# Softmax weights transposed unscaled; the inverse row sums multiplied in after the value product

## The chip, the core and the metric

The kernel runs on one core of a Trainium2 chip. The metric is device time in microseconds (us) of one launch, from several runs of the same program. Beside the times there is one profiled execution, from which the trace and its page come. The engines have short names: PE (matrix products; PEld is its loading of weights), DVE (VectorE), ACT (ScalarE), POOL (GpSimd), SP (the queue that issues nearly all DMAs here). The 16 DMA engines move data between SBUF and DRAM and within SBUF.

## What is computed

The reference is two blocks, both float32, on x of 4 x 1024 x 512: a graph attention over 20 key positions with a ReLU and a residual, and then a conditioned transformer block. The change touches the attention of the second:

```
def _attention(x, W_qkv, W_out, b_out):          # B=4, 16 heads of 64, here 1024 rows
    q, k, v = jnp.split(x @ W_qkv, 3, axis=-1)   # each reshaped to (B, T, 16, 64)
    attn = jnp.einsum('bqhd,bkhd->bhqk', q, k) * DH ** -0.5
    attn = jax.nn.softmax(attn, axis=-1)
    out = jnp.einsum('bhqk,bkhd->bqhd', attn, v).reshape(Bq, Tq, INNER)
    return out @ W_out + b_out
x = x + g_msa * _attention(_modulate(_layernorm(x), sh_msa, sc_msa), W_qkv, W_out, b_out)
x = x + g_mlp * _ff(_modulate(_layernorm(x), sh_mlp, sc_mlp), W1, b1, W2, b2)
```

## The kernel before

There are three stages: the graph attention (to about 408 us), the softmax attention with the projections around it (408 to about 2230 us), and the feed-forward stage. All engines' instructions are emitted by the program in a fixed order; each engine takes its own in that order, and semaphores make it wait where it needs another's result.

The softmax stage is a loop over 256 steps (`for s in range(NS + 1)`). A step is one batch, one pair of heads (`gp`, 8 of them) and one tile `t` of 128 query rows (8 of them). In a step:

- `scores` (L1156): PE writes the scores of the two heads, 128 x 1024 each, into two PSUM tiles `psc`.
- `largest` (L1167): DVE reduces each to its negated row maximum.
- `weights` (L1173): ACT takes the exponential of each into `w`, and the row sums `sm` with it.
- `scaled`: DVE takes the reciprocal of each sum (L1178), and then ACT (head 0, L1180) or POOL (head 1, L1182) multiplies the 128 x 1024 weights by it, in place.
- `turn` (L1191, L1195): DVE transposes the weights in blocks of 32 x 32 into `wd`, and after every second tile SP issues four DMAs of 256 KB for each head, which move the blocks of `wd` between partitions into `wT`. Eight DMAs belong to one block of `QB` = 256 query rows, that is two steps; there are 128 such blocks. `wd` has three slots, and a block takes two of them, one for each head; `wT` has two slots.
- `attend` (L1064, L1076): at least two steps after the second tile, PE multiplies `wT` with the values into the PSUM tile `pav`, and ACT copies `pav` into `oT`, which is the input of the output projection.

The weights of step s are transposed in step s+1: `turn` of head 0 is the first thing that DVE does in it, and `turn` of head 1 stands behind the two maxima and the first reciprocal. Before the maxima stand the evacuations that the step before put off (`later`).

The rest of the step is filled by `emit`. A planner gives every piece of other work (projections to queries, keys and values in seven products, L533; the output projection, L1139 with DVE's additions in L1148; `attend`; loads of weights and rows) a cost and a first and last step, and spreads them so that the steps are about equally long on PE. The planner and its costs are the same in both kernels. Loads (`wqk`, `wv`, `wout`, `xr`, `xl`) and stores (`x2d`) of these pieces go through SP's queue too, in the order of emission. The program waits for a DMA by semaphore on the engine that needs it; where SP needs the landing of a DMA before it issues another, SP waits and so does everything behind it.

Of the kernel before, what the change touches and what calls it, by code (L numbers as in the profile page):

```python
# [12 lines left out]
F32 = mybir.dt.float32  # L13
I32 = mybir.dt.int32
AF = mybir.ActivationFunctionType
ALU = mybir.AluOpType
# [3 lines left out]
P = 128  # L20
S = 1024
F = 512
FC = F // P
NT = S // P
# [8 lines left out]
H, D = 16, 64  # L33
# [8 lines left out]
def cond_block_kernel(  # L42
# [27 lines left out]
    nc = tc.nc  # L70
# [4 lines left out]
    def row(ap):  # L75

        return ap.unsqueeze(0)
# [46 lines left out]

    x1d = [tc.dram_tile([P, F], F32, name=f"x1d{i}") for i in range(NTA)]
    gated = tc.dram_tile([P, F], F32, name="gated")
    qrd = tc.dram_tile([B, F], F32, name="qrd")
    vrd = [tc.dram_tile([KV, F], F32, name=f"vrd{d}") for d in range(2)]
    x2d = [tc.dram_tile([P, F], F32, name=f"x2d{i}") for i in range(NTA)]
# [2 lines left out]
    with ExitStack() as gctx:  # L132
        KC0 = GH * 2 * NG // P
        HF = GH * NG
        gp = gctx.enter_context(tc.tile_pool(name="gp", bufs=1))
# [49 lines left out]
        with ExitStack() as sctx:  # L185
# [13 lines left out]
            rows = sp.tile([N_VEC, P], F32, name="rows")  # L199
# [8 lines left out]
            ws, gboB = [], sp.tile([KV, 2, F], F32, name="gboB")  # L208
# [365 lines left out]
        later = []  # L574
# [366 lines left out]
    with ExitStack() as actx:  # L941
        ap_ = actx.enter_context(tc.tile_pool(name="ap", bufs=1, reuse_waits="tile"))
        q1, q2 = (ps.tile([P, F], F32, name=n, tag=n) for n in ("q1", "q2"))
        two_banks = {"ma": q2, "mb": q1, "mc": q1, "md": q2}
        NP = 2 * NGRP
# [3 lines left out]
        QB = 256  # L949
        QT = QB // P  # L950
        NB = S // QB
        wout, gate = {}, {}
        vt, oT, xr, wn, wd, wT = {}, {}, {}, {}, {}, {}

        turns = []

# [98 lines left out]
        def attend(b, gp, k, a=0, z=KC):  # L1055

            if a == 0:
                pav[0] = ps.tile([P, F], F32, name="pav", tag="pav")[:, :QB]
            po = pav[0]
            g, p = divmod(gp, 2)  # L1060
            w = wT[b, gp, k]
            for m in range(a, z):
                for j in range(2):
                    nc.tensor.matmul(  # L1064
                        po[j * D : (j + 1) * D, :],
                        lhsT=vt[b, g][:, m, p * P + j * D : p * P + (j + 1) * D],
                        rhs=w[:, j, :, m, :],
                        start=(m == 0),
                        stop=(m == KC - 1),
                    )  # L1070
            if z < KC:
                return
            u, i = divmod(k, 2)
            if i == 0:
                oT[b, gp, u] = op_.tile([P, F], F32, name="oT", tag="oT", bufs=6)
            nc.scalar.copy(  # L1076
                oT[b, gp, u][:, i * QB : (i + 1) * QB].rearrange("p (t u q) -> p u t q", t=QT, u=4),
                po.rearrange("p (u t q) -> p u t q", t=QT, u=4),
            )

        def project(b, g, n):
# [69 lines left out]
        def scores(b, gp, t):  # L1151
            sc = [ps.tile([P, S], F32, name="psc", tag="sc", bufs=2) for _ in range(2)]
            for n in range(2):
                for j in range(2):
                    q = slice(j * D, (j + 1) * D)
                    nc.tensor.matmul(  # L1156
                        sc[j][:, n * F : (n + 1) * F],
                        lhsT=qT[b, gp][q, t * P : (t + 1) * P],
                        rhs=kT[b, gp][q, n * F : (n + 1) * F],
                        start=True,  # L1160
                        stop=True,
                    )
            return sc

        def largest(sc):
            mx = ap_.tile([P, 1], F32, name="mx", tag="mx", bufs=4)
            nc.vector.tensor_reduce(mx, sc, axis=AX.X, op=ALU.max, negate=True)  # L1167
            return mx

        def weights(sc, mx):  # L1170
            w = ap_.tile([P, S], F32, name="w", tag="w", bufs=4)
            sm = ap_.tile([P, 1], F32, name="sm", tag="sm", bufs=4)
            nc.scalar.activation(w, sc, AF.Exp, bias=mx, accum_out=sm)  # L1173
            return w, sm

        def scaled(j, w, sm):

            nc.vector.reciprocal(sm, sm)  # L1178
            if j == 0:
                nc.scalar.mul(w, w, sm)  # L1180
            else:
                nc.gpsimd.tensor_scalar(w, w, sm, None, ALU.mult)  # L1182

        def turn(b, gp, t, j):

            k, at = divmod(t, QT)
            if at == 0:
                wd[j] = ap_.tile([P, 4 * KC, QT, U], F32, name="wd", tag="wd", bufs=3)
                if j == 0:
                    wT[b, gp, k] = ap_.tile([P, 2, 4, KC, QT * U], F32, name="wT", tag="wT", bufs=2)  # L1190
            nc.vector.transpose(wd[j][:, :, at, :], wn.pop((b, gp, t, j)).rearrange("p (m k) -> p m k", k=U))  # L1191
            if at == QT - 1:
                flat = wd[j].rearrange("p m t q -> p (m t q)")
                for u in range(4):
                    nc.sync.dma_start(  # L1195
                        wT[b, gp, k][:, j, u].rearrange("p m q -> p (m q)"), flat[U * u : U * (u + 1), :]
                    )
# [11 lines left out]
        def halves():  # L1209

            two = [ps.tile([P, S], F32, name="up", tag="sc", bufs=2) for _ in range(2)]
            return {n: two[k // 2][:, k % 2 * F : (k % 2 + 1) * F] for k, n in enumerate(("ma", "mb", "mc", "md"))}
# [5 lines left out]
        NS = B * NP * NT  # L1218
# [21 lines left out]
        for b in range(B):  # L1240
# [22 lines left out]
            for gp in range(NP):  # L1263
                g, p = divmod(gp, 2)
                at = s0 + gp * NT
# [12 lines left out]
                for k in range(NB):  # L1278
                    lo = at + QT * k + LAG
                    if gp == NP - 2:  # L1280

                        for h in range(2):
                            add(lo + h, lo + h, 1, 1, attend, b, gp, k, h * KC // 2, (h + 1) * KC // 2)
                        continue
                    add(lo, lo + (lo < NS - 8), 2, 1, attend, b, gp, k)
# [60 lines left out]
        for i in range(4):  # L1346
            at = NS - (10, 9, 6, 3)[i]
# [109 lines left out]
        def fill_of(s):  # L1457
            return [k for k in range(len(fill)) if where[k] == s]

        def emit(a, b):  # L1460


            for s in range(a, b):
                steps = {where[k] for k in chain}
                second = [k for k in outs if where[k] == s][1:]

                def place(k):
                    if k in inside:
                        at = 2.5 if s - 1 in steps else 0.5
                        if k in chain:  # L1470
                            return at
                        if k in second:
                            return 3.5
                        return min(at, 2) + 0.1 if s in steps else 2
                    return fill[k][3]

                for k in sorted(fill_of(s), key=lambda k: (place(k), k)):
                    if k not in done_early:
                        fill[k][4]()
                if s in steps and s - 1 not in steps and sum(fill[k][2] for k in fill_of(s)) >= 3:  # L1480
                    while later:
                        later.pop(0)()
# [3 lines left out]
        def early(s):  # L1486

            two = [k for k in outs if where[k] == s]
            sums = [k for k in fill_of(s) if fill[k][3] == -1]
            for k in two[: len(two) - 1] + sums:  # L1490
                fill[k][4]()
                done_early.add(k)

        row_sum(0, 2)
        emit(-3, 0)
        before = None
        for s in range(NS + 1):
            if before is not None:
                turn(*before[0], 0)
            while later:  # L1500
                later.pop(0)()
            if s < NS:
                b, r = divmod(s, NP * NT)
                gp, t = divmod(r, NT)
                sc = scores(b, gp, t)
                mx = [largest(sc[j]) for j in range(2)]
                early(s)
                ws = [weights(sc[j], mx[j]) for j in range(2)]
                now = ((b, gp, t), ws)
                scaled(0, *ws[0])  # L1510
            if before is not None:
                turn(*before[0], 1)
            before = None
            if s < NS:
                scaled(1, *ws[1])
                for j in range(2):
                    wn[(*now[0], j)] = ws[j][0]
                before = now
            if s < NS:
                emit(s, s + 1)  # L1520
        sc_banks = halves()
        late = []
        second = with_four(
# [25 lines left out]
    with ExitStack() as mctx:  # L1549
# [53 lines left out]
        for k in range(NB2):  # L1603
            b = k * VB // NT
# [3 lines left out]
            for p in range(2 if k == 0 else 0, 4):  # L1608
# [12 lines left out]
                elif p == 3:  # L1621
                    sums = []
                    for j in range(2):
                        o = [w2x[j][:, n] for n in range(3)]
                        q, r = w2s[j], w2s[2 + j]
# [97 lines left out]
```

## Time and profile before

| | us |
|---|---|
| runs | 3037.86, 3039.97, 3045.48 |
| median | 3039.97 |
| span of the profiled execution | 3034.2 |
| first softmax step to last exponential | about 408 to 2230 |
| L1182, POOL's scaling pass, 256 of them | 728.6 busy |
| L1180, ACT's scaling pass, 256 of them | 291.0 busy |
| L1178, DVE's reciprocals, 512 of them | 72.5 busy |
| L1076, ACT's copies of `pav`, 128 of them | 0.352 / 0.359 / 0.373 each (least, median, most) |

A group of the page reads: line, engine, operation, what it writes and reads, how many, then busy time and mean ns of one, then the idle time of the engine just before these instructions, and what ended most of it. In a view of waits the first name is the engine and line that waited (SPq is SP's queue), then whom it waited for, then the sum, the count and the longest. The slices of the page for PE's granted clock and for the DMA engines over the whole span, and SP's part of the DMA queues:

```profile
PEclk9999999999999999999999999999999999999999
DMA  6433357777868777768777868766871010101110
...
q1 hardware_dynamic: 282256, 415.03, 53.8%
...
wT<-wd SPq DMA_DIRECT2D x1024, 256.0 KB
```

A digit is a slice of a fortieth of the span. The clock is at full speed throughout, and the DMA engines are busiest in the softmax stage, where the 1024 transfers of `wT` lie.

### The profile page before, as it was taken

How to read it: one execution, taken by the hardware profiler on the slowest of the kernel's cores; microseconds unless marked ns; L12 is line 12 of the kernel's file. 1: busy time of each engine (PE TensorE's matmuls, PEld its weight loads, DVE VectorE, ACT ScalarE, POOL GpSimd, SP SyncE). 2: the span in 40 equal slices, each digit the busy share in tenths (PEclk: the TensorE clock that was granted, in tenths of full speed). 3: DMA queues.
4: the chain of work that ended last, by engine and by line, in shares of the span. 5: the costliest groups of instructions: out<-in, count | busy, mean ns of one | idle time of the engine just before them, and what ended most of it. 6: DMA issues, size and time to landing. Idle time of an engine off the chain costs nothing.

```text
span 3034.2 us, 41780 instructions
## 1 busy us (share of the span) xinstructions
PE 2999.3 (99%) x15317; PEld 1980.2 (65%) x15317; DVE 1999.6 (66%) x2836; ACT 1432.0 (47%) x2368; POOL 1339.4 (44%) x922
## 2 busy tenths in 40 slices
PE   9999999999999999999999999999999999999999
PEld 6666655555555555555555555555568888888888
DVE  3888867777878877878787878877863222222322
ACT  3344456555755565755555755556641221112211
POOL 1444456555656655656655656655721110111010
PEclk9999999999999999999999999999999999999999
DMA  6433357777868777768777868766871010101110
GB/s 201 140 118 121 117 129 180 162 171 179 192 157 210 181 168 179 192 155 211 187 159 180 191 159 205 189 162 164 203 196 63 14 49 28 49 21 35 35 42 15
DMA packets 282695, 417.90 MB, mean 138 GB/s; under 512 B 28968, under 2 KB 101092, under 8 KB 282492
## 3 DMA queue, kind: packets, MB, share of 16 engines
q1 hardware_dynamic: 282256, 415.03, 53.8%
q8 instruction: 123, 2.02, 0.3%
q14 instruction: 80, 0.66, 0.1%
q10 hardware_dynamic: 236, 0.20, 0.0%
HBM read 120.93 MB, written 25.76 MB: 48 GB/s over the span
## 4 chain that ended last, share of the span: by engine, by line
PE 83%; DVE 7%; ACT 3%; POOL 3%; issue 2%; DMA 2%; SPq 1%; POOLq 0%; DVEq 0%; ACTq 0%
PE q L533 19%; PE psc L1156 15%; PE pav L1064 13%; PE pu L1139 6%; PE mbd L533 5%; PE mbu L533 5%; PE mad L533 4%; PE mau L533 3%; PE mcd L533 2%; PE mdd L533 2%; PE mdu L533 2%; PE mcu L533 2%; DVE mx L1167 1%; ACT w L1173 1%; POOL t L742 1%
## 5 line engine op out<-in xcount | busy, mean ns | idle before, releaser
L1182 POOL TENSOR_SCALAR w<-w,sm 128x1024 f32<-128x1024 f32 x256 | 728.6, 2846 | 701.5 <-DVE sm L1178 686.4
L1173 ACT ACTIVATE w<-psc,mx 128x1024 f32<-128x1024 f32 x512 | 570.7, 1115 | 642.6 <-DVE mx L1167 641.6
L1191 DVE STREAM_TRANSPOSE wd<-w 128x1024 f32<-128x1024 f32 x512 | 632.2, 1235 | 109.3 <-ACT w L1180 96.0
L1167 DVE TENSOR_REDUCE mx<-psc 128x1 f32<-128x1024 f32 x512 | 599.2, 1211 | 80.2 <-PE psc L1156 77.0
L1156 PE MATMUL psc<-kT,qT 64*128 64x512 f32 x2048 | 526.9, 615 | 3.1 <-ACT kT L1024 1.4
L1064 PE MATMUL pav<-wT,v 128*64 128x256 f32 x4096 | 482.1, 383 | 1.2 <-DMA wT<-wd 0.6
L1064 PEld LDWEIGHTS pav<-wT,v 128*64 128x64 f32 x4096 | 296.1, 137 | 224.0 <-issue 86.0
L1156 PEld LDWEIGHTS psc<-kT,qT 64*128 64x128 f32 x2048 | 201.6, 186 | 220.5 <-issue 151.2
L1180 ACT ACTIVATE w<-w,sm 128x1024 f32<-128x1024 f32 x256 | 291.0, 1137 | 0.0
L512 POOL TENSOR_TENSOR tx<-hT 128x512 f32<-128x512 f32 x8 | 10.3, 1288 | 596.5 <-ACT hT L448 596.5
L1148 DVE TENSOR_TENSOR xr<-pu,xr 128x512 f32<-128x512 f32 x210 | 143.5, 683 | 78.9 <-PE pu L1139 78.7
L533 PE MATMUL q<-hT,wqk 128*128 128x512 f32 (+1 forms) x396 | 181.2, 581 | 1.0 <-DVE q L547 1.0
L555 ACT COPY mbu<-mau 128x512 f32<-128x512 f32 x30 | 17.1, 570 | 276.5 <-PE mau L533 276.5
L719 PE MATMUL pa<-kp,sfT 128*128 128x320 f32 x512 | 143.5, 433 | 1.4 <-ACT sfT L694 1.4
L533 PEld LDWEIGHTS q<-hT,wqk 128*128 128x128 f32 x396 | 74.7, 190 | 80.9 <-issue 78.2
L533 PE MATMUL q<-tx,ex 128*128 128x512 f32 (+1 forms) x264 | 123.5, 591 | 1.8 <-POOL tx L618 1.3
L719 PEld LDWEIGHTS pa<-kp,sfT 128*128 128x128 f32 x512 | 94.8, 190 | 38.2 <-ACT sfT L694 1.9
L679 PE MATMUL pf<-wx,xT 128*128 128x512 f32 x256 | 116.0, 596 | 0.0
L533 PE MATMUL mad<-w,hs 128*128 128x256 f32 x512 | 113.1, 379 | 0.0
L533 PEld LDWEIGHTS mad<-w,hs 128*128 128x128 f32 x512 | 97.3, 190 | 13.2
L1139 PE MATMUL pu<-wout,oT 128*128 128x256 f32 x360 | 98.4, 396 | 4.2 <-DVE xr L1148 3.7
L1139 PEld LDWEIGHTS pu<-wout,oT 128*128 128x128 f32 x360 | 62.6, 189 | 59.3 <-issue 31.6
(309 smaller groups left out, 4590.7 us busy)
## 6 DMA issues: line engine op xcount, KB each, us to landing
wT<-wd SPq DMA_DIRECT2D x1024, 256.0 KB
wqk<-in_w_qkv SPq DMA_DIRECT2D x64, 256.0 KB
xT<-in_xt SPq DMA_DIRECT2D x32, 256.0 KB
xs<-in_x SPq DMA_DIRECT2D x32, 256.0 KB
x1d<-xs SPq DMA_DIRECT2D x32, 256.0 KB
xl<-x1d SPq DMA_DIRECT2D x32, 256.0 KB
wv<-in_w_qkv SPq DMA_DIRECT2D x32, 256.0 KB
xr<-x1d SPq DMA_DIRECT2D x32, 256.0 KB
```

The source lines that it names most:

```text
L533: nc.tensor.matmul(t[:, q * width : (q + 1) * width], lhsT=lhs(which, q, k), rhs=rhs(which, q, k), start=(fresh and q == 0 and k == 0), st ...
L679: nc.tensor.matmul(pfs[i], lhsT=xT[i][:, c, :], rhs=wx[:, c, :], start=False, stop=(c == FC - 1), skip_group_check=True,)
L719: nc.tensor.matmul(pas[i][:, n, :HF], lhsT=sfT2[i][:, c, :], rhs=kp[:, b, c, n * HF : (n + 1) * HF], start=False, stop=(c == FC - 1), skip ...
L1064: nc.tensor.matmul(po[j * D : (j + 1) * D, :], lhsT=vt[b, g][:, m, p * P + j * D : p * P + (j + 1) * D], rhs=w[:, j, :, m, :], start=(m == 0),
L1139: nc.tensor.matmul(pu[0][:, q * HB : (q + 1) * HB], lhsT=a[:, q * P : (q + 1) * P], rhs=r, start=(bool(fresh) and q == 0), stop=True, skip ...
L1148: nc.vector.tensor_tensor(o, pu[0].rearrange("p (r f) -> p r f", r=2), o, ALU.add)
L1156: nc.tensor.matmul(sc[j][:, n * F : (n + 1) * F], lhsT=qT[b, gp][q, t * P : (t + 1) * P], rhs=kT[b, gp][q, n * F : (n + 1) * F], start=Tru ...
L1167: nc.vector.tensor_reduce(mx, sc, axis=AX.X, op=ALU.max, negate=True)
L1173: nc.scalar.activation(w, sc, AF.Exp, bias=mx, accum_out=sm)
L1180: nc.scalar.mul(w, w, sm)
L1182: nc.gpsimd.tensor_scalar(w, w, sm, None, ALU.mult)
L1191: nc.vector.transpose(wd[j][:, :, at, :], wn.pop((b, gp, t, j)).rearrange("p (m k) -> p m k", k=U))
```

## The change

The weights keep their raw exponentials. The scaling passes are gone. The row sums of the two tiles and two heads of a block gather in one tile of 128 x 4; after the second tile DVE inverts them in one instruction (`scales_out`) and SP stores them to DRAM, turned, as four rows of 128. In the next step SP reads them back (`scales_in`), once for each head, as a row of 256 spread over that head's 64 partitions, into `rB`. `attend` then leaves PSUM by a DVE multiplication with `rB` instead of an ACT copy. The transposes move too: `turn` of both heads now stands in the same step, behind the exponentials, and `w` has two slots instead of four.

```diff
+    scd = [tc.dram_tile([4, P], F32, name=f"scd{i}") for i in range(4)]
...
-            nc.scalar.copy(
+            nc.vector.tensor_tensor(
                 oT[b, gp, u][:, i * QB : (i + 1) * QB].rearrange("p (t u q) -> p u t q", t=QT, u=4),
                 po.rearrange("p (u t q) -> p u t q", t=QT, u=4),
+                rB.pop((b, gp, k)).rearrange("p (t u q) -> p u t q", t=QT, u=4),
+                ALU.mult,
             )
...
-        def weights(sc, mx):
-            w = ap_.tile([P, S], F32, name="w", tag="w", bufs=4)
-            sm = ap_.tile([P, 1], F32, name="sm", tag="sm", bufs=4)
-            nc.scalar.activation(w, sc, AF.Exp, bias=mx, accum_out=sm)
-            return w, sm
-        def scaled(j, w, sm):
+        def weights(b, gp, t, j, sc, mx):
+            k, at = divmod(t, QT)
+            w = ap_.tile([P, S], F32, name="w", tag="w", bufs=2)
+            if (b, gp, k) not in esum:
+                esum[b, gp, k] = ap_.tile([P, 2 * QT], F32, name="sm", tag="sm", bufs=2)
+            c = j * QT + at
+            nc.scalar.activation(w, sc, AF.Exp, bias=mx, accum_out=esum[b, gp, k][:, c : c + 1])
+            wn[b, gp, t, j] = w
+        def scales_out(b, gp, k):
+            sm = esum.pop((b, gp, k))
             nc.vector.reciprocal(sm, sm)
-            if j == 0:
-                nc.scalar.mul(w, w, sm)
-            else:
-                nc.gpsimd.tensor_scalar(w, w, sm, None, ALU.mult)
+            spot[0] += 1
+            scales[b, gp, k] = scd[spot[0] % len(scd)]
+            nc.sync.dma_start(scales[b, gp, k].rearrange("c p -> p c"), sm)
+        def scales_in(b, gp, k):
+            rows = scales.pop((b, gp, k))
+            rB[b, gp, k] = ap_.tile([P, QB], F32, name="rB", tag="rB", bufs=2)
+            for j in range(2):
+                nc.sync.dma_start(
+                    rB[b, gp, k][j * D : (j + 1) * D, :],
+                    row(rows[j * QT : (j + 1) * QT, :].rearrange("t q -> (t q)")).broadcast_to([D, QB]),
+                )
...
-        for s in range(NS + 1):
-            if before is not None:
-                turn(*before[0], 0)
+        for s in range(NS):
             while later:
                 later.pop(0)()
...
+            for j in range(2):
+                weights(b, gp, t, j, sc[j], mx[j])
+            for j in range(2):
+                turn(b, gp, t, j)
+            while coming:
+                scales_in(*coming.pop())
+            if t % QT == QT - 1:
+                scales_out(b, gp, t // QT)
+                coming.append((b, gp, t // QT))
+            emit(s, s + 1)
```

More of the change, by code (lines that the diff above doesn't have):

```diff
@@ L953, in cond_block_kernel @@
         vt, oT, xr, wn, wd, wT = {}, {}, {}, {}, {}, {}
+        esum, scales, rB, spot = {}, {}, {}, [0]
         turns = []
@@ L1495, in cond_block_kernel @@
         emit(-3, 0)
-        before = None
-        for s in range(NS + 1):
-            if before is not None:
-                turn(*before[0], 0)
+        coming = []
+        for s in range(NS):
             while later:
                 later.pop(0)()
[L1502 to L1520, printed above, removed]
+            b, r = divmod(s, NP * NT)
+            gp, t = divmod(r, NT)
+            sc = scores(b, gp, t)
+            mx = [largest(sc[j]) for j in range(2)]
+            early(s)
+            for j in range(2):
[8 more added lines that the diff above has]
+            emit(s, s + 1)
+        while later:
+            later.pop(0)()
+        scales_in(*coming.pop())
         sc_banks = halves()
```

## The prediction

> **What bounds the kernel now.** I read the busy shares first, then the attention stage by itself, then who waits there.
>
> ```profile
> PE 2999.3 (99%) x15317; PEld 1980.2 (65%) x15317; DVE 1999.6 (66%) x2836; ACT 1432.0 (47%) x2368; POOL 1339.4 (44%) x922
> ...
> PE 83%; DVE 7%; ACT 3%; POOL 3%; issue 2%; DMA 2%; SPq 1%; POOLq 0%; DVEq 0%; ACTq 0%
> ...
> L1182 POOL TENSOR_SCALAR w<-w,sm 128x1024 f32<-128x1024 f32 x256 | 728.6, 2846 | 701.5 <-DVE sm L1178 686.4
> L1191 DVE STREAM_TRANSPOSE wd<-w 128x1024 f32<-128x1024 f32 x512 | 632.2, 1235 | 109.3 <-ACT w L1180 96.0
> L1167 DVE TENSOR_REDUCE mx<-psc 128x1 f32<-128x1024 f32 x512 | 599.2, 1211 | 80.2 <-PE psc L1156 77.0
> L1180 ACT ACTIVATE w<-w,sm 128x1024 f32<-128x1024 f32 x256 | 291.0, 1137 | 0.0
> ```
>
> PE is the bound everywhere. The two scaling passes that the change deletes are large (728.6 us of POOL, 291.0 us of ACT) but lie on engines that idle half the time. The stage that the change touches is the softmax loop, 408 to 2230 us, 256 steps; its own sums (the view of busy time by stretch):
>
> ```profile
> 408.00:2230.00 1822.00, 1807.45 (x9769) 1030.80 (x9770) 1467.91 (x1900) 1096.76 (x1708) 1104.56 (x716) 1.00 0.75 180
> ```
>
> The columns are length, then PE, PEld, DVE, ACT, POOL, clock, DMA share, GB/s. PE idles 14.6 us in 1822. That is all there is to win, whatever is taken off other engines. A step is 1822/256 = 7.12 us; a block of two steps (one `wT`) is 14.2 us. DVE is busy 5.73 us of a step; the DMA engines are busy 75% of the time, which no other engine's row tells. So I looked at the queue that feeds them, SP's waits over the whole kernel, then what DVE waits for:
>
> ```profile
> SPq L1195 <- DVE wd L1191: 498.4, 124, 9.3
> ...
> SPq L363 <- DMA vrd<-vrow: 5.6, 2, 3.9
> ...
> SPq L313 <- DMA qrd<-qrows: 1.7, 1, 1.7
> ```
> ```profile
> DVE wd L1191 <- ACT w L1180: 95.2, 118, 0.9
> ...
> DVE wd L1191 <- DMA wT<-wd: 3.9, 6, 0.9
> ```
>
> The first line is SP's spare time: in 124 of 128 blocks it has issued everything and waits for the next transposes, 498.4 us in all. With the 19.4 us of its wait for L1178 that is 518/128 = 4.05 us a block. The second and third are the only places where a tensor is stored to DRAM and read back at once: SP, which issues in order, stands still for 1.7 to 3.9 us each time. The last shows that six transposes had to wait, up to 0.9 us, for a `wd` slot whose DMAs had not landed.
>
> **The change part by part.**
>
> *Removed.* 256 ACT passes of 1.137 us, 256 POOL passes of 2.846 us, 512 reciprocals (72.5 us of DVE). All of it lies beside PE. ACT's L1180 pass also holds up transposes (95.2 us) and the ACT copies behind it, but PE's own waits in the stage are the 14.6 us. Gain: 0 to 14.6 us; I take 0, because the terms below eat it.
>
> *Moved to DVE.* 128 evacuations of `pav` were ACT copies of 0.359 us; as multiplications with one PSUM operand they cost between 0.34 us (half of L1148, 128x512, 0.683 us) and 0.683 us; I take 0.4: 51 us. 128 reciprocals of four columns at 0.14 us: 18 us. DVE changes by -72.5 + 51 + 18 = -3 us. Nothing.
>
> *Transposes one step earlier.* Both transposes of step s now follow its maxima instead of standing in step s+1. The maxima lose the transpose ahead of them (1.24 us) and the exponentials behind get ready before DVE needs them: maximum 1.21, exponential 1.11 beside the second maximum. In return the distance between the transposes that fill a `wd` slot and the one that reuses it shrinks. Three slots serve two a block, so (block k+1, head 1) reuses (k, head 0). Before, from the end of the one to the start of the other was a step plus two maxima and a reciprocal, 7.1 + 2.6 = 9.7 us; after, just a step, 7.1 us. By the semaphore updates in the trace the fourth of the four DMAs lands 7.75 us after the first is issued (median of 127 blocks). So DVE waits 0.65 us in every other step, when SP is on time; its idle 1.4 us a step covers that. If SP is late, DVE is late by as much, and with it the next maxima, exponentials and scores.
>
> *Three more DMAs a block on SP, one of which waits.* The order of SP's queue in the changed kernel is: eight `wT`, the store of the sums (512 pieces of 4 B), loads that fall in the odd step, two broadcasts back (64 x 1 KB), loads that fall in the even step, the next eight `wT`. The broadcasts wait for the store to land, and everything behind them on SP waits too: next come loads and the `wT` transfers that DVE's slots and PE's `attend` need.
> - Eight `wT`: first issue to the end of the last, 8.79 us (mean; 8.5 to 9.1 for eight blocks in ten). Unloaded they would take 0.55 us each; they are paced by the DMA engines.
> - Issue of the store to its landing. The trace has no store of 4 B pieces. Low end: `x1d` stores in the first stage, with an empty queue, 2.0 us. In the softmax stage, behind `wT`: `x2d` stores 4.96 us median, `wT` itself 4.75. Pieces: loads of 512 pieces send their first semaphore 0.5 us later than loads of 128 (3.57 against 3.05). 4.96 + 0.5 = **5.5 us**. High end: each 4 B piece priced as a slow 2 KB packet, 130 ns (mean in the stage), 512 x 0.13/16 = 4.2 us, so about 9.2 us. Small packets in the trace take 9 to 12 ns (4 to 128 B), which is why I stay near the low end for the pieces.
> - Two broadcasts: 0.43 us issue and 0.05 us between, 1.0 us.
> - Of some 200 loads in the stage 102 fall between store and broadcasts, inside the wait: 102 x 0.86 us / 128 = 0.7 us hidden.
>
> So the change asks SP for 5.5 + 1.0 - 0.7 = 5.8 us more a block and it has 4.05. Deficit 1.75 us x 127 blocks = **220 us**. Doing the same block by block, each with its own length in this trace and its own trailing loads at 0.86 us (next block's `wT` start no earlier than this one's broadcasts; PE allowed to run 1 to 3 us ahead of DVE), gives 217 us. DMA engine time itself grows little: 0.3 us for the pieces and 128 x 46 ns/16 = 0.4 us for the broadcasts, on 14.2.
>
> The page "DMA: Bandwidth & Descriptors" of the Trainium skill, section "Rules for kernel authors", speaks against this store: a last dimension with a stride becomes one descriptor per element, and a transpose by a rearranged access pattern is put at a 19x difference. If I apply that to 0.3 us of pieces, an estimate of 5.4 us more for each store and some 690 us more in all; no row here shows it.
>
> Sum against the profiled execution: 3034.2 + 220 = 3254; the median of the runs lies 5.8 us above the span, so **3260 us**.
>
> **The rivals.**
> 1. *The store lands within SP's spare time (not slower).* If store to landing takes 3.75 us or less (5.5 less the 1.75 of deficit), SP is on time. The read-back waits of 1.7 to 3.9 us, taken outside the crowded stage, speak for it; the 4.96 us of stores inside it against it. What then remains is DVE: either its slack hides the slot waits and PE's idle time shrinks, up to 14.6 us, 3025 us; or nothing moves, 3040.
> 2. *SP is on time but the slots decide.* Store in 2.5 to 3.75 us, with some blocks short of SP's mean spare time (a tenth have under 0.6 us) and 0.65 us of DVE wait in each. The block-by-block sum gives 15 to 80 us: 3085.
> 3. *The scatter is slow.* Store to landing 8 us: SP needs 2.5 us more a block, 127 x 4.25 = 540 us: 3580. At 9.2 us it is 700 us.
>
> **How the numbers follow.** Forecast (store 4.5 to 6.5 us, so +90 to +350) 0.50; rival 2, 0.20; rival 3 (+350 and more) 0.15; rival 1, 0.15, half of it faster by over 0.3%, half within 0.3% (9 us, about what a measurement of this kernel can tell from no change). So faster 0.08, same 0.07, slower 0.85. The range leaves out rival 1 for the most part, at the low end, and the slower half of rival 3: 3055 to 3540.
>
> **What would show it.** SP's wait for `wd` falls from 498 us to under 100, and in its place stand waits of the broadcast line for the store of the sums, 3 to 4 us each, 128 of them. DVE's transposes wait for `wT` transfers for over 150 us in all, instead of 3.9. PE idles 200 us or more in the stage, its busy time unchanged; the stage grows from 1822 to some 2040 us and the DMA share falls from 0.75 to about 0.70. POOL's busy time drops by 729 us and ACT's by 337, without use. Wrong, if SP still waits for `wd` for over 250 us (rival 1 or 2), or if the broadcasts wait over 6 us each (rival 3). The stages before 408 and after 2230 us must not change.

## The result, and the profile after

The changed kernel takes 3684.51 us (median of four runs, 3673.98 to 3694.07) against 3038.91 us for the kernel before (four runs, 3037.43 to 3045.48). The ratio is 1.2122, with a 95% interval of 1.2101 to 1.2144: 646 us slower. The forecast was 3260 us, and its range ended at 3540.

The profiled execution spans 3672.1 us. From its page: the busy shares, the granted clock by fortieths of the span, and the chain that ended last, by engine and by line.

```profile
PE 3226.2 (88%) x15317; PEld 2047.7 (56%) x15317; DVE 1997.5 (54%) x2580; ACT 1121.3 (31%) x1984; POOL 613.5 (17%) x666
...
PEclk9999989898898989889889989888998999999999
...
PE 31%; SPq 26%; DMA 25%; DVE 7%; issue 6%; POOL 2%; ACT 1%; DVEq 0%; POOLq 0%; ACTq 0%
SPq L1212 22%; DMA scd<-sm 20%; DMA wT<-wd 5%; PE mbd L534 5%; PE mbu L534 4%; PE psc L1160 3%; PE mad L534 3%; SPq L1196 3%; PE mau L534 3%; DVE mx L1171 2%; PE q L534 2%; PE pav L1066 2%; PE mcd L534 2%; PE mdd L534 2%; PE mdu L534 1%
```

PE's share of the chain fell from 83% to 31%. Half of the chain is now SP and the DMAs, and two things make up most of that: SP issuing `wT` (L1212, 22%) and the landing of the sums in DRAM (`scd<-sm`, 20%). POOL and ACT got their time back (POOL 1339 to 614 us, ACT 1432 to 1121), without use.

The softmax stage now ends near 2868 us instead of 2230; the stage before it is as long as it was, and so is the one behind (from the last exponential to the end 805.9 us before, 807.1 now). The stage by itself, with the columns of the prediction's view (length, PE, PEld, DVE, ACT, POOL, clock, DMA share, GB/s):

```profile
408.00:2868.00 2460.00, 2035.98 (x9781) 1099.88 (x9780) 1467.92 (x1646) 787.90 (x1329) 381.23 (x462) 0.90 0.61 140
```

DVE's work is what it was to a tenth (1467.91 before, 1467.92 now). PE idles 424 us, and its "busy" time itself grew by 229 us. SP's waits in the stage, then DVE's, then the group of the new evacuation:

```profile
SPq L1196 <- DMA scd<-sm: 852.1, 127, 8.4
SPq L1212 <- DVE wd L1208: 10.9, 5, 8.0
```
```profile
DVE wd L1208 <- DMA wT<-wd: 795.9, 126, 9.8
```
```profile
L1078 DVE TENSOR_TENSOR oT<-pav,rB 128x256 f32<-128x256 f32 x128 | 49.7, 388 | 18.4 <-PE pav L1066 9.7 <-DMA rB<-scd 8.7
```

SP used to wait for the transposes (498.4 us); that is 10.9 us now, and in its place stand 127 waits of 6.7 us each (mean) for the store of the sums. The prediction had named waits over 6 us as the sign of its rival 3. DVE, held up for 3.9 us by `wT` transfers before, now waits 796 us for them. One round of SP, from the timeline of its queue (start, length, line, operation):

```profile
1216.42 7.38 SPq L1212 DMA_DIRECT2D wT<-wd  x6
1223.91 0.53 SPq L1189 DMA_DIRECT2D scd<-sm  x1
1224.56 1.89 SPq L457 DMA_DIRECT2D wv<-in_w_qkv  x2
1231.48 1.12 SPq L1196 DMA_DIRECT2D rB<-scd  x2
1232.70 8.60 SPq L1212 DMA_DIRECT2D wT<-wd  x8
```

The store is issued at 1223.91 and the first broadcast can go only at 1231.48. By the semaphore updates, a store takes 8.4 us (mean; median 8.2) from its issue to its landing. A round is eight `wT` at 8.8 us, the landing at 8.4, two broadcasts at 1.25 and the loads behind them at 0.6: 19.1 us. The stage has 128 rounds, and from the first exponential to the last it takes 2452.5 us, which is 19.2 us each.

### The profile page after: what moved, and what is told of

Read it like the earlier page. It is cut to its first block, busy times and chain, and to the rows that moved or that the text cites. A ratio compares the mean times of both kernels' runs of the same rounds, so it can differ in the third digit from the quotient of the medians.

```text
span 3672.1 us, 41728 instructions
## 1 busy us (share of the span) xinstructions
PE 3226.2 (88%) x15317; PEld 2047.7 (56%) x15317; DVE 1997.5 (54%) x2580; ACT 1121.3 (31%) x1984; POOL 613.5 (17%) x666
## 4 chain that ended last, share of the span: by engine, by line
PE 31%; SPq 26%; DMA 25%; DVE 7%; issue 6%; POOL 2%; ACT 1%; DVEq 0%; POOLq 0%; ACTq 0%
SPq L1212 22%; DMA scd<-sm 20%; DMA wT<-wd 5%; PE mbd L534 5%; PE mbu L534 4%; PE psc L1160 3%; PE mad L534 3%; SPq L1196 3%; PE mau L534 3%; DVE mx L1171 2%; PE q L534 2%; PE pav L1066 2%; PE mcd L534 2%; PE mdd L534 2%; PE mdu L534 1%
## 5 line engine op out<-in xcount | busy, mean ns | idle before, releaser
L1208 DVE STREAM_TRANSPOSE wd<-w 128x1024 f32<-128x1024 f32 x512 | 621.0, 1232 | 878.5 <-DMA wT<-wd 795.9
L1160 PE MATMUL psc<-kT,qT 64*128 64x512 f32 x2048 | 639.0, 698 | 128.9 <-ACT w L1180 126.6
L1066 PE MATMUL pav<-wT,v 128*64 128x256 f32 x4096 | 502.4, 398 | 0.2 <-issue 0.2
L1160 PEld LDWEIGHTS psc<-kT,qT 64*128 64x128 f32 x2048 | 235.4, 212 | 411.4 <-issue 206.1
L534 PE MATMUL q<-hT,wqk 128*128 128x512 f32 (+1 forms) x396 | 201.4, 636 | 52.9 <-DVE q L548 52.9
L1143 PE MATMUL pu<-wout,oT 128*128 128x256 f32 x360 | 118.1, 458 | 117.6 <-DVE xr L1152 117.6
L1143 PEld LDWEIGHTS pu<-wout,oT 128*128 128x128 f32 x360 | 71.0, 217 | 179.9 <-DVE xr L1152 99.4
L505 POOL TENSOR_TENSOR ex<-wqk 128x256 f32<-128x256 f32 x33 | 24.0, 727 | 824.8 <-PE q L534 344.3
L1152 DVE TENSOR_TENSOR xr<-pu,xr 128x512 f32<-128x512 f32 x210 | 140.3, 668 | 19.4 <-PE pu L1143 19.2
L1143 PE MATMUL pu<-wsum,osum 128*128 128x256 f32 x240 | 71.8, 425 | 38.0 <-DVE xr L1152 37.8
L975 POOL TENSOR_TENSOR wout<-wout,gate 128x512 f32<-128x512 f32 x32 | 39.8, 1266 | 390.5 <-DMA wout<-in_w_out 390.5
```

Of the source, the lines that this page charges most:

```text
L534: nc.tensor.matmul(t[:, q * width : (q + 1) * width], lhsT=lhs(which, q, k), rhs=rhs(which, q, k), start=(fresh and q == 0 and k == 0), st ...
L1066: nc.tensor.matmul(po[j * D : (j + 1) * D, :], lhsT=vt[b, g][:, m, p * P + j * D : p * P + (j + 1) * D], rhs=w[:, j, :, m, :], start=(m == 0),
L1143: nc.tensor.matmul(pu[0][:, q * HB : (q + 1) * HB], lhsT=a[:, q * P : (q + 1) * P], rhs=r, start=(bool(fresh) and q == 0), stop=True, skip ...
L1152: nc.vector.tensor_tensor(o, pu[0].rearrange("p (r f) -> p r f", r=2), o, ALU.add)
L1160: nc.tensor.matmul(sc[j][:, n * F : (n + 1) * F], lhsT=qT[b, gp][q, t * P : (t + 1) * P], rhs=kT[b, gp][q, n * F : (n + 1) * F], start=Tru ...
```

## The experiments

My theory after the result: SP's in-order queue is the bound, because the 512 pieces of 4 B land late. Its rivals: the early transposes and their slots; PE's clock, which no longer holds full speed; and harm that the store does to other transfers without anybody waiting for it. Each edit is against the changed kernel, if nothing else is said; each ratio is to the kernel before, on the same chip.

**1. No store and no read-back.** The multiplier is a constant.

```diff
-            nc.sync.dma_start(scales[b, gp, k].rearrange("c p -> p c"), sm)
...
-            rB[b, gp, k] = ap_.tile([P, QB], F32, name="rB", tag="rB", bufs=2)
...
+            rB[b, gp, k] = one
```

> No store and no broadcasts: the values are multiplied by a constant tile on leaving PSUM, so the division by the sums is left out. What is left is the early transposes, the missing scaling passes and the evacuation by DVE. Theories W and B: 3025 to 3060 us, transposes waiting for wT some 0.65 us in every other step. Rival S (the early transposes run into their three slots and this alone slows the loop): over 3120 us.

Measured: 3076.31 us, ratio 1.0120 (1.0104 to 1.0136), between the two expectations. The three DMAs carry 608 of the 646 us. The other 38 us are what the rest of the change costs, less what it gains. DVE's first wait in this kernel is

```profile
DVE wd L1204 <- DMA wT<-wd: 200.7, 123, 3.4
```

That is 1.6 us in nearly every block; experiment 7 shows what it is worth.

**2. The store kept, nobody waits for it.** The broadcasts read the slot that was stored two blocks earlier, so the output is scaled by other rows' sums.

```diff
+            at = scd[spot[0] % len(scd)]
+            scales[b, gp, k] = scd[(spot[0] - 2) % len(scd)] if spot[0] > 2 else at
+            nc.sync.dma_start(at.rearrange("c p -> p c"), sm)
```

> The store keeps its 512 pieces, but the broadcasts read the slot that was stored two blocks earlier, which has long landed (the scales are another block's). No wait for the store is left on SP; all transfers stay. Theory W: 3040 to 3100 us. Rival B (the pieces hold up the DMA engines themselves for some 4 to 5 us, whoever waits): a block needs 10.7 us of DMA time as before plus 4.5 and the broadcasts, over 15 us against 14.2, so 3150 to 3250 us.

Measured: 3315.07 us, ratio 1.0913 (1.0897 to 1.0930), more than both theories expected. The wait of the broadcasts is worth 3684.5 - 3315.1 = 369 us. But 277 us remain with no such wait, 239 more than without the DMAs, though SP has spare time again:

```profile
SPq L1213 <- DVE wd L1209: 282.1, 113, 8.2
```

So SP's wait is not the whole cost of these DMAs.

**3. The same store, alone, in the kernel before.** One a block, of constants, which nobody reads. Against the kernel before:

```diff
+                if j == 1:
+                    spot[0] += 1
+                    nc.sync.dma_start(scd[spot[0] % len(scd)].rearrange("c p -> p c"), four)
```

> The kernel before, with one store of 512 pieces of 4 B (of a constant tile) to DRAM behind the eight wT transfers of each block, that nobody reads or waits for. Theory W: 3035 to 3060 us. Rival B: SP's spare time of 4.05 us a block is used up and wT lands later, 3100 us or more.

Measured: 3255.27 us, ratio 1.0726 (1.0702 to 1.0750): 217 us for 128 stores of 2 KB that nothing depends on. PE's first wait, and DVE's wait for the same transfers:

```profile
PE pav L1069 <- DMA wT<-wd: 100.7, 41, 7.3
```
```profile
DVE wd L1196 <- DMA wT<-wd: 70.0, 31, 6.8
```

Behind 72 of the 128 stores SP issues another transfer within 2 us. By the semaphore updates that next transfer lands 10.2 us (median) after its own issue. One such place, from the timeline of SP's queue, and the view of busy time for three stretches behind the store:

```profile
1324.75 0.59 SPq L1205 DMA_DIRECT2D scd<-four  x1
1325.45 1.92 SPq L457 DMA_DIRECT2D wqk<-in_w_qkv  x2
1327.93 10.25 SPq L1200 DMA_DIRECT2D wT<-wd  x8
```
```profile
1325.00:1328.00 3.00, 3.00 (x16) 1.80 (x14) 2.86 (x5) 3.00 (x6) 2.02 (x1) 1.00 0.79 184
1328.00:1334.50 6.50, 6.17 (x34) 3.29 (x34) 6.40 (x9) 3.63 (x6) 3.28 (x2) 1.00 0.28 39
1334.50:1338.00 3.50, 3.40 (x24) 1.80 (x23) 2.43 (x4) 2.84 (x5) 3.19 (x5) 1.00 0.99 350
```

The last two columns are the reading. For 6.5 us the DMA engines are busy 28% and move 39 GB/s, though two loads of 256 KB and the first `wT` transfers are in the queue; then they are busy 99% and move 350 GB/s. The packet records show the 4 B packets, 9 ns each, nearly all begun before 1328; then the 512 B packets of the loads come slowly, and the first 2 KB packet of the queued `wT` starts at 1335. The store costs next to no engine time that shows as busy, and what stands behind it is late. Experiment 6 has the comparison.

The profile puts 43.2 us of SP's own waits down to this store too (29 times, at the issue of `wT`), though no data binds the two. In all 29 the waiting transfer is the eighth that SP issues behind the store, and it tells its landing on the same semaphore: in this program SP's DMAs take eight semaphores in turn.

**4. The sums stored as they lie.** 128 pieces of 16 B instead of 512 of 4 B; the broadcasts wait as in the changed kernel.

```diff
+    scd = [tc.dram_tile([P, 4], F32, name=f"scd{i}") for i in range(4)]
...
+            nc.sync.dma_start(scales[b, gp, k], sm)
...
+                    row(rows[j * D : (j + 1) * D, :].rearrange("p c -> (p c)")).broadcast_to([D, QB]),
```

The multipliers then arrive in another order than the queries; the work is the same.

> The sums are stored as they lie, 128 pieces of 16 B, instead of turned in 512 pieces of 4 B; as many bytes are read back, so the scales go to the wrong rows. Everything else as after the change. Theory W (SP stands still until the store has landed, and the landing takes 8.2 us because of its 512 pieces): store to landing falls to about 5 us, a block on SP to 8.8 + 5 + 1.2 + 0.7 = 15.7 us, so about 3230 us. Rival Q (the landing is long because the store stands behind eight transfers of 256 KB): landing stays at 8 us, time stays near 3680 us.

Measured: 3133.09 us, ratio 1.0308 (1.0292 to 1.0323), theory W's way and 97 us below its number. The stage's stores land in 3.7 us (median) instead of 8.2, and SP's wait shrinks to a third:

```profile
SPq L1196 <- DMA scd<-sm: 272.4, 125, 4.0
```

With the same wait on the same path, 551 of the 646 us are gone. They belong to the form of the store, not to the fact that SP waits for one.

**5. Which property of the form.** A probe in the last stage of the kernel before, where SP's queue is nearly empty: six forms of store, each followed by a small read of it, eight times.

```diff
+            nc.sync.dma_start(prb["a"].rearrange("c p -> p c"), four)
+            nc.sync.dma_start(prb["b"], four)
+            nc.sync.dma_start(prb["c"].rearrange("c p -> p c"), pq[:, :1])
+            nc.sync.dma_start(prb["d"][:, :, 0].rearrange("c p -> p c"), four)
+            nc.sync.dma_start(prb["e"], pq)
+            nc.sync.dma_start(prb["f"][:, :, 0], four)
```

> The kernel before; in its last stage, where the DMA engines are nearly idle, six stores of a constant tile to DRAM are made one after the other in each of eight rounds, each followed by a read-back, so that SP's wait for the read-back line shows the landing of that form alone. a: 512 pieces of 4 B turned as in the change (128 in a row per column); b: 128 pieces of 16 B; c: 128 pieces of 4 B, one column turned; d: as a, but the pieces 64 B apart in DRAM; e: 128 pieces of 128 B; f: 512 pieces of 4 B 64 B apart, in the order of the partitions. Theory N (the count of pieces sets the landing): a, d and f alike, 6 to 8 us, b, c and e alike, 2 to 3 us. Rival L (pieces that share a short stretch of DRAM hold each other up): a long, d and f short. Rival Z (the size below some bound): a, b, c, d and f all longer than e.

Measured: 3044.13 us in one run. From issue to landing (median of eight):

```
a  512 x 4 B, adjoining in DRAM, turned (the change's form)   9.2 us
c  128 x 4 B, adjoining, one column                           7.2
d  512 x 4 B, 64 B apart, turned                              2.6
f  512 x 4 B, 64 B apart, in the order of partitions          2.1
b  128 x 16 B, adjoining                                      1.8
e  128 x 128 B, adjoining                                     1.4
```

SP's waits for them say the same (sum, count, longest):

```profile
SPq L1609 <- DMA pra<-pq: 72.5, 8, 13.1
SPq L1613 <- DMA prc<-pq: 54.9, 8, 7.2
...
SPq L1615 <- DMA prd<-pq: 18.1, 8, 2.7
```

A quarter of the pieces (c) is nearly as slow as all of them (a); all 512 pieces, 64 B apart (d, f), are fast. So neither the number of the pieces nor their size alone sets the price. Pieces of 4 B that lie side by side in DRAM do. Pieces between 4 and 16 B, and distances between 4 and 64 B, were not tried.

**6. Experiment 3 with the pieces 64 B apart**, to try that in the crowded stage:

```diff
+    scd = [tc.dram_tile([4, P, 16], F32, name=f"scd{i}") for i in range(4)]
...
+                    nc.sync.dma_start(scd[spot[0] % len(scd)][:, :, 0].rearrange("c p -> p c"), four)
```

> The kernel before with the store of 512 pieces of 4 B that nobody waits for, as in the run with the store alone (3255 us), but the pieces 64 B apart in DRAM. Theory L (pieces that share a short stretch of DRAM hold each other and the transfers behind them up): the store lands in about 4 us and the time is 3035 to 3060 us. Rival N (the count of pieces): near 3255 us.

Measured: 3042.58 us, ratio 1.0015 (1.0006 to 1.0024). The same 512 pieces from the same place in the queue cost 4 us instead of 217. They land in 4.1 us (8.8 to 9.0 in experiment 3), and PE waits 2.3 us for `wT` instead of 100.7. The next transfer, issued within 2 us behind 74 of the stores, lands 4.5 us after its issue (median) instead of 10.2. The same 6.5 us as in experiment 3, counted from the issue of a store with two loads of `wqk` behind it:

```profile
1318.20:1324.70 6.50, 6.50 (x52) 4.10 (x49) 4.92 (x7) 5.12 (x9) 3.63 (x2) 1.00 0.90 234
```

The DMA engines are busy 90% here, and 28% there.

**7. Experiment 1 with four `wd` slots**, for the 38 us of the rest of the change (the constant is one column here, read again for each query):

```diff
-                wd[j] = ap_.tile([P, 4 * KC, QT, U], F32, name="wd", tag="wd", bufs=3)
+                wd[j] = ap_.tile([P, 4 * KC, QT, U], F32, name="wd", tag="wd", bufs=4)
```

> As the run without store and broadcasts (a constant in place of the inverse sums, so the division is left out), with four slots for wd instead of three: a transpose reuses a slot two blocks old. Theory S (the 38 us that this version is slower than before come from transposes that wait for wT): the 200.7 us of that wait go, and the time is 3025 to 3042 us. Rival (the order itself, transposes behind the exponentials, costs): the time stays near 3076 us.

Measured: 3015.38 us, ratio 0.9919 (0.9906 to 0.9931), below what theory S expected. DVE's 200.7 us of waits for `wT` are gone from its list, and 61 us of time with them. This kernel leaves the division out, and it is 25 us faster than the kernel before, more than the 14.6 us that PE idled there. Its stage:

```profile
408.00:2210.00 1802.00, 1791.95 (x9769) 1012.84 (x9769) 1472.15 (x1642) 790.70 (x1327) 381.61 (x462) 1.00 0.75 182
```

PE idles 10.0 us in it, only 4.6 less than before. The larger part is PE's busy time, 1807.45 before and 1791.95 here, for the same products: `psc` took 526.9 us and takes 519.8, `pav` 474.3 and 466.5, while one product took as long as before (615 and 383 ns). So part of what the view called busy was probably waiting.

**8. Four `wd` slots in the changed kernel itself**, with the edit of 7 (the tile `gates` moves to another pool, to make room):

> The changed kernel with four slots for wd. Theory W (SP's own round, eight transfers, the store's landing and the broadcasts, is the bound): within 25 us of the changed kernel's 3684 us, though the transposes no longer wait. Rival S (the slots pass SP's lateness on to DVE and so to PE, and more room takes it away): 3600 us or less.

Measured: 3676.83 us, ratio 1.2089 (1.2064 to 1.2113), so the slots, worth 61 us in 7, are worth some 8 us here. DVE's wait for slots goes, and another takes its place; SP's stays:

```profile
SPq L1196 <- DMA scd<-sm: 872.5, 128, 8.6
```
```profile
PE pav L1066 <- DMA wT<-wd: 240.9, 93, 9.7
```

It also decides about the clock. By the clock's records PE had half speed for 517 us in the changed kernel and for 401 us here, with nearly the same time. So the lower clock is not the bound.

**9. A store of whole rows.** The sums are turned on DVE first (blocks of 32 x 32) and stored as 128 pieces of 128 B, and the broadcasts read 256 B pieces. It is the full computation.

```diff
+            smT = ap_.tile([P, U], F32, name="smT", tag="smT", bufs=2)
+            nc.vector.transpose(smT, sm)
...
+            nc.sync.dma_start(scales[b, gp, k], smT)
```

> The whole computation, with the sums turned on DVE before they are stored: the four columns lie in a 128x32 tile, DVE transposes it in 32x32 blocks, the store is 128 pieces of 128 B, and the two broadcasts read pieces of 256 B. Position and waits as in the change. Theory N: landing near 4 us as with 16 B pieces (3.7 us), 3110 to 3150 us. Rival Z (small pieces of 16 B are fast for another reason): over 3200 us.

Measured: 3149.48 us, ratio 1.0362 (1.0345 to 1.0380). The store lands in 3.7 us, no sooner than 16 B pieces; behind nothing, in experiment 5, this form took 1.4. SP still waits for it:

```profile
SPq L1203 <- DMA scd<-smT: 262.5, 124, 3.7
```

**10. The same, with the store ahead of half the `wT`.** Sums and broadcasts are issued between head 0's and head 1's transfers.

```diff
+            turn(b, gp, t, 0)
             while coming:
                 scales_in(*coming.pop())
             if t % QT == QT - 1:
                 scales_out(b, gp, t // QT)
                 coming.append((b, gp, t // QT))
+            turn(b, gp, t, 1)
```

> As the run with the turned store, and the store stands on SP between the four wT transfers of head 0 and those of head 1, so that the second four are issued while it lands. Theory W: SP's wait for the store, near 270 us, falls below 60 us, and the time comes down to that of the run without store, 3075 to 3095 us. Rival (SP's queue has no room for three more DMAs at all): no better than the run with the turned store.

Measured: 3075.01 us, ratio 1.0110 (1.0095 to 1.0125). SP's list has no wait for the store left, and the time is that of experiment 1, which has no store at all.

**11. The same with four `wd` slots** (room for them: the tile `gates` moved to another pool).

> The whole computation: the turned store between the two heads' transfers, and four slots for wd (the room comes from a tile of the first stage that no longer lives through the kernel). Theory (what is left of the loss is the slot waits, 61 us between the two runs without store): 3015 to 3035 us, below before. Rival (SP's three DMAs a block still cost): 3040 us or more.

Measured: 3043.22 us, ratio 1.0014 (1.0005 to 1.0023), as the rival said. That takes back all but 4 us of the 646, and is still no faster than the kernel before. Against experiment 7 the three DMAs and the division cost 28 us: PE idles 23.5 us in 408 to 2230, and 10.0 there in 408 to 2210.

**12. Norm rows one step later.** In 11, ACT took up norms of `xl` rows late and pushed scores and exponentials behind; the planner's dates for them are moved by a step.

```diff
-                        ((-18, (-15, -14, -14, -13), -12), (-10, (-9, -9, -8, -8), -7))
+                        ((-18, (-15, -14, -14, -13), -12), (-10, (-8, -8, -8, -8), -7))
```

> As the run with four slots and the turned store between the heads (3043 us), and ACT's first two normalisations of the second half of a batch's rows stand one step later, so that ACT no longer waits 6 us for their loads, which come later on SP than before the change. The trace of the run before it showed two such stalls end in PE idle for 1.6 to 1.7 us and then in 6 us at half the granted clock. Theory: these go, 5 to 12 us less, 3030 to 3039 us. Rival (four normalisations in one step delay its exponentials as much): 3043 us or more.

Measured: 3045.52 us, ratio 1.0020 (1.0011 to 1.0030), no better than 11. ACT's two waits for these rows (6.0 and 5.9 us) went, and near the same two places PE waited for `wT` (2.3 and 1.7 us) and for a product of POOL, `tx` (2.0 and 2.5 us), instead. No version with the full computation beat the kernel before; what the last 28 us are, one by one, stays open.

## Why the prediction was wrong

- **The path was right.** PE was the bound; SP became it; the broadcasts wait for the store on SP, and DVE waits for `wT` behind them; the stages outside did not move; the evacuation costs 0.388 us (0.4 said) and DVE's sum is unchanged.
- **The step that failed: "4.96 + 0.5 = 5.5 us" from the store's issue to its landing.** It is 8.4 us. Of its two terms the place in the queue was put too high and the pieces far too low: with 16 B pieces at the same place a store lands in 3.7 us (experiment 4), so the place is worth 3.7 and not 4.96, and the 4 B pieces 4.7 and not 0.5. The 0.5 came from loads, which write to SBUF; no row of the profile before had small pieces written side by side to DRAM. The range should have given the two ends of the landing, 2.0 and 9.2 us, more equal weight.
- **What the right number gives.** With 8.4 us the prediction's own sum is (5.8 + 2.9 - 4.05) x 127 = 590 us, so 3034 + 590 = 3624 against a span of 3672. Of the 48 us that are left some 32 are the broadcasts, 1.25 us for two instead of 1.0.
- **Rival 3** (the scatter is slow; 540 us for 8 us, 700 for 9.2; chance 0.15) is what happened. Its price for the high end, 130 ns for each piece, was near by luck: it counts pieces, and form f of experiment 5 has as many and lands in 2.1 us.
- **"DMA engine time itself grows little"** is true of busy time and wrong as a price. Experiment 3 shows 217 us with nobody reading the store, by transfers that are late behind it. The sum had no term for what the store does to others. How much of that falls together with SP's wait in the changed kernel is not shown.
- **The rule of the Trainium skill** that the prediction weighed ("DMA: Bandwidth & Descriptors", "Rules for kernel authors": one descriptor per element, 19x for a transpose by access pattern) led to an estimate of some 690 us, close to the 646, but by chance. Its ground, the count of the descriptors, is not what costs here: form f has the 512 pieces and lands in 2.1 us, form c has 128 and takes 7.2. It warned of the right store for a reason that these runs contradict.
- **"Its idle 1.4 us a step covers that"** (three `wd` slots) failed too: DVE waits 1.6 us a block and not 0.65, and it is not covered; experiment 7 against 1 makes it 61 us. In the changed kernel most of it is hidden under SP's round (experiment 8).
- **"PE idles 200 us or more in the stage, its busy time unchanged"**: the idle time is 424 us, and the busy time did not stay: it grew by 229 us (the last section says what is known).
- **"That is all there is to win"** (14.6 us) was too low: 25 us were there without the division. PE's busy time, with its modelled ends, probably holds waits.

The 646 us, each part on top of the one before it: 38 for the rest of the change with its slot waits (1), 239 for the store and the broadcasts with nobody waiting for the store (2), 369 for SP's wait for it. In another order the shares would differ, as 7 and 8 show for the slots.

## What to carry to other kernels

When a small store to DRAM is added to a queue in use, ask first how its pieces lie in DRAM: pieces of 4 B side by side, as a turned store of a column writes them, make the transfers behind them late. Spaced 64 B apart, the same pieces cost 4 us where nobody waited for them (6); turned on an engine first, they landed in 3.7 us instead of 8.4 (9). A read-back on an in-order queue is priced from issue to last landing behind what is already queued, and here it cost 74 us less between the large transfers (10) than behind them (9). Where an engine is busy 99%, the sum of its idle gaps is not always the upper limit of the gain (7).

## What the runs showed of the hardware

- While neighbouring 4 B pieces land, the DMA engines are mostly idle with work in the queue (0.28 and 39 GB/s for 6.5 us, against 0.90 and 234 GB/s with the pieces 64 B apart), so a view of busy shares shows the harm as free time. Why adjoining 4 B pieces take so long to be acknowledged, these runs don't show; 16 B pieces, four to a stretch of 64 B, landed in 1.8 us.
- The more PE waited in these runs, the longer the granted clock was at half speed, by the clock's records: 2.9 us in the kernel before (PE idle 14.6 us in the stage), 22 in experiment 11 (23.5), 139 in 3, 230 in 2, 517 in the changed kernel (424). `psc` products took 698 ns each there, and 615 before, so part of the 229 us of added "busy" PE time is slower clock. The Trainium skill ("TensorE: Matmul & The Clock Gate", "HAM oscillation — how this bites in real kernels") puts the limit at idle gaps of about 3.4 us. In experiment 11 a piece of 6.8 us at half speed began at 806 us, behind a shown gap of 1.72 us:

```profile
803.95 4.05 PE L1164 MATMUL psc<-kT,qT 64*128 64x512 f32 x8 [1.72 <-ACT w L1184]
```

Since ends are modelled, the true gap may be longer than the trace shows.
